# One scan over both values of a step instead of one for each, with doubled decay rows

## The chip, the cores and the metric

The kernel runs on one core of a Trainium2 chip. The time is the device time of one execution in microseconds (us); the figure given for a kernel is the median of its runs. The engines are called as in the profile: PE (TensorE, matrix products and transposes), DVE (VectorE), ACT (ScalarE), POOL (GpSimd, which here also starts the gathers and the weight loads) and SP (SyncE, which starts most other transfers). Each engine works through its own instructions in order.

## The reference, cut to what matters

The program computes two layers. Layer 0 adds to its input a mixer and a mixture of experts. The mixer, for B = 8 batches, T = 512 tokens and 16 heads of 16 keys by 16 values, is a recurrence that runs forward and backward over the tokens:

```python
def fwd_step(S, inp):
    rt, kt, vt, wt = inp
    S = jnp.exp(wt)[..., None] * S + kt[..., None] * vt[..., None, :]
    return (S, jnp.einsum('bhk,bhkv->bhv', rt, S))
def bwd_step(S, inp):
    rt, kt, vt, wt = inp
    y = jnp.einsum('bhk,bhkv->bhv', rt, S)
    S = jnp.exp(wt)[..., None] * (S + kt[..., None] * vt[..., None, :])
    return (S, y)
...
y = (y_f + y_b)   # then a gate, a norm over each head, a product with g and with Wo
```

The decay exp(wt) depends on batch, token and key, but not on the value index. Layer 1 (attention and a second mixture of experts) follows; no part of it is changed.

## The kernel before, in words

**The scans.** The state is laid out with 128 rows on the partitions (8 heads of 16 keys, two such halves c for the 256 keys of a batch) and the 512 tokens along the free axis. For one value index, a row is a linear recurrence along the tokens, which DVE's `tensor_tensor_scan` computes: out[t] = data0[t] * out[t-1] + data1[t]. The forward and the backward recurrence are joined: a first scan runs forward with factors `dq`, and a second runs over its result from the end with the factors `d`; `dq`, `d`, `q` and a changed `k` are made so that what comes out is the sum of both states.

**A step** (function `scans`) treats NV = 2 values of one half c of one batch; there are 8 x 2 x 8 = 128 steps. It multiplies the two value rows, which a transfer has spread over the partitions (`spread`, tile kv, 128 x 2 x 512, four buffers), by k (L901), scans each of the two rows forward (L910) and backward (L914), multiplies by r (L923), and leaves to PE the sum over the keys (L929, into the bank ys), which is issued for two steps at a time.

**Decays.** For each batch, `decays` computes d on ACT (two Exp, L829 and L830, 128 x 2 x 512 with one zero column behind each row), q on DVE (L835, L836), near on ACT (Ln L841, Exp L843) and dq on DVE (L848 to L854), and then multiplies k by q (L858). d and dq have two buffers each, so that the next batch's can be made while this one's are read.

**Order.** DVE, PE, ACT and SP take their instructions in the order in which the program issues them. That order is made by taking turns: every piece of work is a Python generator, and `Turns.turn` lets each issue its instructions up to its next `yield`. A step of the scans has four turns: L901; the two scans of the first row (and perhaps the sums for PE); the two scans of the second; L923. In the same turns the experts of layer 0 (39 chunks; g and u products L615, h on ACT L639 and on DVE L624, y L655, the turned inputs xsT L587 and L601), the projections and decays of the next batch (products m L732 and L734, their use xf on DVE L739 and POOL L742, the Ws L697) and the ending of the last one (L942 on: yg L950, yc L954, sq L957, var L965, sd L971 and L973, wide L976, rs L982, z L985 to L987, o L997) issue theirs. POOL's order is set by the scheduler instead. POOL also starts the weight loads wgu and wdn (L567), which wait until PE is done with the buffer, and the gathers xs (L577).

**Buffers in the way of the change.** `held(i, ...)` gives the tiles of a pool of numbered places with one buffer each. Places 0 to 7 first hold the normed inputs xn0 to xn7, later parts of the routing: `turn_round` makes for each of eight k a pair ls, hs (DVE L550, ACT L556) for PE's products L538 in four places each; batch 0's near lies in places 4 and 5. Layer 1 uses them again. PE's results of the projections, and the ending's var and rs, come out of the pool ps_rw with two banks; g, u, xsT and y out of ps_gu with four.

Of the kernel before, what the change touches and what calls it, by code (L numbers as in the profile page):

```python
# [26 lines left out]
F32 = mybir.dt.float32  # L27
I32 = mybir.dt.int32
AF = mybir.ActivationFunctionType
ALU = mybir.AluOpType  # L30
# [6 lines left out]
P = 128  # L37
# [128 lines left out]
def two_layers(ctx: ExitStack, tc: tile.TileContext, a: dict, out: bass.AP):  # L166
# [10 lines left out]
    def held(i, shape, name):  # L177
        return hold.tile(shape, F32, tag=f"held{i}", name=name)
# [193 lines left out]
    with ExitStack() as l0:  # L372
# [142 lines left out]
        def turn_round():  # L515


            n2 = NCH * NS
            parts = rw.tile([P, 5, NTT], F32, tag="x", name="parts")
            low, high, number = parts[:, 0:2], parts[:, 2:4], parts[:, 4]  # L520
            low, high = [[w[:, i] for i in range(2)] for w in (low, high)]
            whole = rw.tile([P, NTT], I32, tag="th", name="whole")
            for i in range(2):
                vec_e.tensor_scalar(whole, slot[i], P - 1, None, ALU.bitwise_and)
                vec_e.tensor_copy(low[i], whole)
                vec_e.tensor_scalar(whole, slot[i], 7, None, ALU.arith_shift_right)
                vec_e.tensor_copy(high[i], whole)
            vec_e.tensor_scalar(
                number, C["count"][:, :NTT], float(P), C["part"], ALU.mult, ALU.add
            )  # L530
            yield
            inv = ps_e.tile([P, n2], F32, tag="e", name="inv")
            last = None
            for k in range(NTT // 4 + 1):
                if last:
                    for j in range(4):
                        for i in range(2):
                            pe.matmul(  # L538
                                inv, last[0][:, i, j, :], last[1][:, i, j, :],
                                start=k == 1 and i + j == 0,  # L540
                                stop=k == NTT // 4 and (i, j) == (1, 3),
                            )
                    last = None
                if k < NTT // 4:
                    ls = held(k % 4, [P, 2, 4, P], f"ls{k}")
                    hs = held(4 + k % 4, [P, 2, 4, n2], f"hs{k}")
                    for i in range(2):
                        for o, of in ((ls, low), (hs, high)):
                            n = o.shape[3]
                            vec_e.tensor_tensor(  # L550
                                o[:, i], bc(of[i][:, 4 * k : 4 * k + 4], 2, n),
                                bc(C["count"][:, :n], 1, 4), ALU.is_equal,
                            )
                    for j in range(4):
                        n = 4 * k + j
                        act_e.activation(  # L556
                            hs[:, :, j, :], hs[:, :, j, :], AF.Copy, scale=number[:, n : n + 1]
                        )
                    last = ls, hs
                yield  # L560
            vec_e.tensor_copy(whose, inv)
            yield
# [106 lines left out]

        made = {}  # L670

        def projections(b):


# [13 lines left out]
            def mix(name, i, other=False):  # L688
                if other and first:
                    return held(i, [P, T], f"{name}_{b}")  # L690
                return rw.tile([P, T], F32, tag="xf", name=f"{name}_{b}", bufs=4)

            def project(w, xs, co, name, bank=bank):

# [111 lines left out]

            def decays():
                yield from until("inputs", b)
                d = rw.tile([P, NC, T + 1], F32, tag="d", name=f"d_{b}", bufs=2)
                vec_e.memset(d[:, :, T:], 0.0)  # L810
                dT = d[:, :, :T]
                xw, xr = yield from mixed(0, 3, other=True)
                ps = other_bank("dw")
                for c in range(NC):
                    pe.matmul(ps[:64, :], dw1[:, c, :], xw[c], start=c == 0, stop=c == NC - 1)
                yield
                act_e.activation(th[:64, :], ps[:64, :], AF.Tanh)
                r, pss = yield from projected(xr, 0, "r", other_bank)
                for co in range(NC):
                    act_e.copy(r[:, co, :], pss[co])  # L820
                pss = []
                for co in range(NC):
                    pss.append(other_bank(f"w{co}"))
                    pe.matmul(
                        pss[co], dw2[:, co * P : (co + 1) * P], th[:64, :], start=True, stop=True
                    )
                yield
                for co in range(NC):
                    act_e.activation(dT[:, co, :], pss[co], AF.Exp, bias=V("time_decay", co))  # L829
                act_e.activation(dT, dT, AF.Exp, scale=-1.0)  # L830
                for _ in range(1 if first else 2):
                    yield

                q = rw.tile([P, NC, T + 1], F32, tag="v", name=f"q_{b}", bufs=2)
                vec_e.tensor_scalar(q, d, 1.0, -1e-12, ALU.subtract, ALU.min)  # L835
                vec_e.scalar_tensor_tensor(q, d, 1.0, q, ALU.add, ALU.mult)  # L836
                yield

                near = [mix(f"near{c}", 4 + c, True) for c in range(NC)]
                for c in range(NC):  # L840
                    act_e.activation(near[c], q[:, c, :T], AF.Ln, scale=-1.0)  # L841
                for c in range(NC):
                    act_e.activation(near[c], near[c], AF.Exp, scale=-1.0)  # L843
                for _ in range(1 if first else 2):
                    yield
                dq = big("dq")
                for c in range(NC):
                    vec_e.tensor_tensor(dq[:, c, :], q[:, c, :T], near[c], ALU.mult)  # L848
                    vec_e.scalar_tensor_tensor(
                        dq[:, c, :], dq[:, c, :], 2.0, near[c], ALU.add, ALU.mult  # L850
                    )
                yield
                vec_e.scalar_tensor_tensor(dq, dq, -1.0, q[:, :, 1:], ALU.mult, ALU.mult)
                vec_e.tensor_tensor(dq, dq, dT, ALU.mult)  # L854
                yield
                yield from until("keys", b)
                k = made[b]["k"]
                vec_e.tensor_tensor(k, k, q[:, :, 1:], ALU.mult)  # L858
                made[b].update(d=d, dq=dq, r=r)
                done.add(("scans", b))  # L860
                yield
                (xg,) = yield from mixed(4)
                g, pss = yield from projected(xg, 3, "g")
                for co in range(NC):
                    act_e.activation(g[:, co, :], pss[co], AF.Silu)
                made[b]["g"] = g

            return inputs(), values(), decays()

        NV = 2  # L870
        STEPS = P // (P // HD) // NV

        def spread(b, c, vg):

            kv = rw.tile([P, NV, T], F32, tag="kv", name=f"kv{c}{vg}_{b}", bufs=4)
            for hh in range(P // HD):
                row = c * P + hh * HD + vg * NV
                nc.sync.dma_start(  # L878
                    kv[hh * HD : (hh + 1) * HD], bc(made[b]["vd"][row : row + NV, :], 0, HD)
                )  # L880
            return kv

# [2 lines left out]
        def scans(turns):  # L887
# [4 lines left out]
            for n, (b, c, vg) in enumerate(todo):  # L892
                if c == vg == 0:
                    x = rw.tile([P, NT, D], F32, tag="x", name=f"x_{b}")
                    z = rw.tile([P, NC, T], F32, tag="z", name=f"z_{b}")
                    if b + 1 < B:
                        turns.add(then(*projections(b + 1)))
                k, d, dq, r = (made[b][n] for n in ("k", "d", "dq", "r"))
                dc, qc, kc, rc = d[:, c, 1:], dq[:, c, :], k[:, c, :], r[:, c, :]
                kv = kvs.pop((b, c, vg))  # L900
                vec_e.tensor_tensor(kv, kv, bc(kc, 1, NV), ALU.mult)  # L901
                if vg == 0:
# [3 lines left out]
                if n + 1 == len(todo):  # L906
                    done.add(("spread",))
                yield
                for i in range(NV):
                    vec_e.tensor_tensor_scan(  # L910
                        out=kv[:, i, :], data0=qc, data1=kv[:, i, :], initial=0.0,
                        op0=ALU.mult, op1=ALU.add,
                    )
                    vec_e.tensor_tensor_scan(  # L914
                        out=kv[:, i, ::-1], data0=dc[:, ::-1], data1=kv[:, i, ::-1],
                        initial=0.0, op0=ALU.mult, op1=ALU.add,
                    )
                    if i == 0 and len(late) == 2:
                        for sums in late:
                            sums()  # L920
                        late = []
                    yield
                vec_e.tensor_tensor(kv, kv, bc(rc, 1, NV), ALU.mult)  # L923

                def sums(b=b, c=c, vg=vg, kv=kv, y=y, z=z, x=x):
# [618 lines left out]
```

## Time and profile before

| | us |
|---|---:|
| Median of 3 runs (2727.06 to 2733.11) | 2727.75 |
| The profiled execution | 2728.59 |
| Its span, first to last instruction | 2726.8 |
| DVE busy / PE busy / ACT busy / POOL busy in the span | 2157.0 / 2362.4 / 888.3 / 477.5 |
| First scan, last scan (start) | 99.8, 1421.2 |
| Scans L910 and L914 (512 of them), busy | 656.7 |
| The multiplies L901 and L923 (256 of them), busy | 334.9 |

The durations all come from the one profiled execution, so sums are made against its 2728.59 us. The scans fill about the first half of the execution, together with the experts of layer 0; after about 1480 us layer 1 runs. In the rows of the profile, "idle before" is the time in which an engine stood still ahead of a group of instructions, with what ended the wait; a busy PE is not PE at its peak, because the ends of its instructions are modelled.

### The profile page before, as it was taken

To read this page: it belongs to the slowest core of one execution; us is meant where nothing else is said; L and a number is where in the kernel's file an instruction comes from. 1 tells how busy PE (TensorE), PEld (TensorE's weight loads), DVE (VectorE), ACT (ScalarE), POOL (GpSimd) and SP (SyncE) were. 2 spreads that over 40 slices of the span, in tenths; PEclk is the share of its full clock that TensorE was granted. 3 is DMA by queue.
4 is the path that set the end of the run, shared out by engine and by line. 5 is a ranking of instruction groups with operands and counts; after the bars stand their busy time and mean duration, and the time that the engine had idled before them with its cause. 6 is when DMAs were issued, how large, how long until landed. Compare 5 with 4: busy or idle time off the path is not lost.

```text
span 2726.8 us, 32763 instructions
## 1 busy us (share of the span) xinstructions
PE 2362.4 (87%) x11900; PEld 1412.8 (52%) x11900; DVE 2157.0 (79%) x3063; ACT 888.3 (33%) x1687; POOL 477.5 (18%) x441
## 2 busy tenths in 40 slices
PE   6699898988989889898826899999989989898996
PEld 4355555555556545555503445555555555555554
DVE  7799999899999989989985755656576675756666
ACT  1233232222323123231102334434333434434344
POOL 2132232322223223232012100010010101001000
PEclk9688998989889899999957899999989989998998
DMA  6335455455465544655443100000010111000000
GB/s 219 112 104 148 141 176 148 142 146 156 138 176 153 158 133 138 173 151 140 138 122 104 43 16 17 20 27 25 20 36 20 32 32 31 25 24 21 20 9 17
DMA packets 100832, 248.87 MB, mean 91 GB/s; under 512 B 24992, under 2 KB 50368, under 8 KB 95552
## 3 DMA queue, kind: packets, MB, share of 16 engines
q1 hardware_dynamic: 70528, 113.32, 15.0%
q0 software_dynamic: 21168, 115.75, 13.6%
q10 hardware_dynamic: 8976, 17.69, 1.8%
q8 instruction: 96, 1.57, 0.2%
q14 instruction: 64, 0.52, 0.1%
HBM read 215.22 MB, written 31.46 MB: 90 GB/s over the span
## 4 chain that ended last, share of the span: by engine, by line
PE 57%; DVE 25%; DMA 6%; issue 6%; ACT 2%; SPq 2%; POOL 1%; DVEq 0%; ACTq 0%; POOLq 0%
PE y L1427 6%; PE y L655 6%; PE g L1381 5%; DMA kv<-vd 5%; PE g L615 4%; PE u L1381 4%; PE u L615 4%; DVE kv L910 3%; PE sc_g L1279 2%; DVE kv L901 2%; PE ys L929 2%; PE o_g L1307 2%; DVE kv L914 2%; PE qkv_l L1171 2%; SPq L878 2%
## 5 line engine op out<-in xcount | busy, mean ns | idle before, releaser
L914 DVE TENSOR_TENSOR_SCAN kv<-d,kv 128x512 f32<-128x512 f32 x256 | 336.7, 1315 | 8.8
L655 PE MATMUL y<-wdn,h 128*128 128x256 f32 x936 | 286.6, 443 | 54.9 <-DVE h L624 50.5
L910 DVE TENSOR_TENSOR_SCAN kv<-dq,kv 128x512 f32<-128x512 f32 x256 | 320.0, 1250 | 3.4
L655 PEld LDWEIGHTS y<-wdn,h 128*128 128x128 f32 x936 | 180.6, 211 | 186.6 <-issue 83.5
L1287 ACT ACTIVATE pt_g<-sc_g 128x512 f32<-128x512 f32 (+1 forms) x384 | 171.2, 531 | 275.0 <-PE sc_g L1279 215.3
L615 PE MATMUL g<-xsT,wgu 128*128 128x256 f32 x936 | 229.2, 388 | 4.7 <-ACT h L639 3.2
L1381 PE MATMUL g<-xT,w 128*128 128x512 f32 x384 | 203.7, 656 | 25.9 <-DVE att_l L1335 14.0
L615 PEld LDWEIGHTS g<-xsT,wgu 128*128 128x128 f32 x936 | 176.1, 192 | 57.4 <-issue 27.4
L1381 PE MATMUL u<-xT,w 128*128 128x512 f32 x384 | 188.5, 614 | 10.7 <-ACT qkT_g L1239 6.0
L615 PE MATMUL u<-xsT,wgu 128*128 128x256 f32 x780 | 196.3, 392 | 0.0
L1427 PE MATMUL y<-w,h 128*128 128x256 f32 x768 | 183.6, 392 | 0.7 <-ACT qkT_g L1239 0.7
L901 DVE TENSOR_TENSOR kv<-kv,k 128x1024 f32<-128x1024 f32 x128 | 172.0, 1344 | 6.6 <-DMA kv<-vd 6.6
L615 PEld LDWEIGHTS u<-xsT,wgu 128*128 128x128 f32 x780 | 149.5, 195 | 51.4 <-issue 22.8
L923 DVE TENSOR_TENSOR kv<-kv,r 128x1024 f32<-128x1024 f32 x128 | 162.9, 1273 | 3.6
L929 PE MATMUL ys<-kv,cst 128*32 128x512 f32 x512 | 105.7, 701 | 65.4 <-DVE kv L923 65.1
L1399 DVE TENSOR_TENSOR h<-h,u 128x512 f32<-128x512 f32 x96 | 66.0, 688 | 121.5 <-PE u L1381 116.6
L1427 PEld LDWEIGHTS y<-w,h 128*128 128x128 f32 x768 | 144.4, 193 | 34.2 <-issue 11.2
L639 ACT ACTIVATE h<-g 128x512 f32<-128x512 f32 (+1 forms) x117 | 61.7, 527 | 272.6 <-PE g L615 262.5
L1293 DVE TENSOR_TENSOR pt_g<-pt_g,cst 128x512 f32<-128x512 f32 x128 | 85.2, 686 | 75.1 <-ACT pt_g L1287 75.1
L742 POOL TENSOR_TENSOR xf<-xf,xnT 128x512 f32<-128x512 f32 x80 | 113.3, 1436 | 124.1 <-DVE xf L739 123.8
L1381 PEld LDWEIGHTS g<-xT,w 128*128 128x128 f32 x384 | 72.6, 201 | 110.7 <-issue 84.8
L1287 ACT ACTIVATE pt_l<-sc_l 128x384 f32<-128x384 f32 (+1 forms) x256 | 98.0, 469 | 86.3 <-PE sc_l L1279 70.7
(307 smaller groups left out, 3874.5 us busy)
## 6 DMA issues: line engine op xcount, KB each, us to landing
kv<-vd SPq DMA_DIRECT2D x1024, 64.0 KB
cb<-cd SPq DMA_DIRECT2D x128, 128.0 KB
outs<-ys POOLq DMA_DIRECT2D x39, 256.0 KB
w<-in_w ACTq DMA_DIRECT2D x12, 384.0 KB
xn<-in_x SPq DMA_DIRECT2D x8, 512.0 KB
xnT<-xT ACTq DMA_DIRECT2D x16, 256.0 KB
normed<-xn SPq DMA_DIRECT2D x8, 512.0 KB
xnT<-xnT SPq DMA_DIRECT2D x8, 512.0 KB
```

The lines of the kernel that those rows point to most:

```text
L615: pe.matmul(o, w[:, at + c * P : at + (c + 1) * P], xT[:, c, :], start=c == 0, stop=c == NC - 1,)
L655: pe.matmul(y[:, n, :], hs[j // 2][lo:, j % 2, n * P : (n + 1) * P], wd[lo:, j * D : (j + 1) * D], start=j == 0, stop=j == NJ0,)
L742: pool_e.tensor_tensor(t, t, xT[c], ALU.add)
L901: vec_e.tensor_tensor(kv, kv, bc(kc, 1, NV), ALU.mult)
L910: vec_e.tensor_tensor_scan(out=kv[:, i, :], data0=qc, data1=kv[:, i, :], initial=0.0, op0=ALU.mult, op1=ALU.add,)
L914: vec_e.tensor_tensor_scan(out=kv[:, i, ::-1], data0=dc[:, ::-1], data1=kv[:, i, ::-1], initial=0.0, op0=ALU.mult, op1=ALU.add,)
L923: vec_e.tensor_tensor(kv, kv, bc(rc, 1, NV), ALU.mult)
L929: pe.matmul(y[r0 : r0 + 32, :], C["take"][:, 24 - 8 * at : 56 - 8 * at], kv[:, i, :], start=at == 0, stop=at == 3, skip_group_check=True,)
L1287: act_e.activation(pt[:, i, :end], scs[i][:, :end], AF.Exp, scale=0.25)
L1293: vec_e.tensor_tensor(pt[:, :, a0 : a0 + m], pt[:, :, a0 : a0 + m], bc(mask[:, :m], 1, 4), ALU.mult,)
L1381: pe.matmul(ps, w[:, k, c * P : (c + 1) * P], xT[:, c, :], start=c == 0, stop=c == NC - 1,)
L1427: pe.matmul(y[:, i, :], hs[k][:, (t + i) * P : (t + i + 1) * P], w1[j - 5 + k][:, 2, :], start=k == 0, stop=k == 5,)
```

## The change

For each half c, the factor rows are copied twice, one behind the other, into tiles of 128 x 2 x 512 (`ds` from d, `dqs` from dq), by ACT. The kv tile of a step is then taken as one row of 1024, and one scan goes forward over it and one backward. Where the second value begins, the factor has to be zero: for the backward scan it is d's zero column, for the forward one POOL writes a zero into the first column of dq. The step keeps four turns: L901, the forward scan, the backward scan, L923. To make room, d and dq have one buffer each, ls and hs two places each, batch 0's near lies in places 0 and 1, and ds and dqs lie in places 4 to 7 for even batches, and in places 1 and 2 and two tiles of their own for odd ones.

```diff
                 if k < NTT // 4:
-                    ls = held(k % 4, [P, 2, 4, P], f"ls{k}")
-                    hs = held(4 + k % 4, [P, 2, 4, n2], f"hs{k}")
+                    ls = held(k % 2, [P, 2, 4, P], f"ls{k}")
+                    hs = held(2 + k % 2, [P, 2, 4, n2], f"hs{k}")
...
+            def twice(name):
+                out = []
+                for c in range(NC):
+                    n = 2 * (name == "dqs") + c
+                    if b % 2 == 0:
+                        out.append(held(4 + n, [P, NV, T], f"{name}{c}_{b}"))
+                    elif n < 2:
+                        out.append(held(1 + n, [P, NV, T], f"{name}{c}_{b}"))
+                    else:
+                        out.append(rw.tile([P, NV, T], F32, tag=f"dqs{c}", name=f"{name}{c}_{b}"))
+                return out
...
-                d = rw.tile([P, NC, T + 1], F32, tag="d", name=f"d_{b}", bufs=2)
+                d = rw.tile([P, NC, T + 1], F32, tag="d", name=f"d_{b}")
...
                 act_e.activation(dT, dT, AF.Exp, scale=-1.0)
+                ds = twice("ds")
+                for c in range(NC):
+                    act_e.copy(ds[c], bc(d[:, c, 1:], 1, NV))
...
-                near = [mix(f"near{c}", 4 + c, True) for c in range(NC)]
+                near = [mix(f"near{c}", c, True) for c in range(NC)]
...
-                dq = big("dq")
+                dq = big("dq", 1)
...
                 vec_e.tensor_tensor(dq, dq, dT, ALU.mult)
-                yield
+                pool_e.memset(dq[:, :, 0:1], 0.0)
+                yield
+                dqs = twice("dqs")
+                for c in range(NC):
+                    act_e.copy(dqs[c], bc(dq[:, c, :], 1, NV))
                 yield from until("keys", b)
...
-                for i in range(NV):
-                    vec_e.tensor_tensor_scan(
-                        out=kv[:, i, :], data0=qc, data1=kv[:, i, :], initial=0.0,
-                        op0=ALU.mult, op1=ALU.add,
-                    )
-                    vec_e.tensor_tensor_scan(
-                        out=kv[:, i, ::-1], data0=dc[:, ::-1], data1=kv[:, i, ::-1],
-                        initial=0.0, op0=ALU.mult, op1=ALU.add,
-                    )
-                    if i == 0 and len(late) == 2:
-                        for sums in late:
-                            sums()
-                        late = []
-                    yield
+                flat = kv.rearrange("p v t -> p (v t)")
+                vec_e.tensor_tensor_scan(
+                    out=flat, data0=qc, data1=flat, initial=0.0, op0=ALU.mult, op1=ALU.add
+                )
+                if len(late) == 2:
+                    for sums in late:
+                        sums()
+                    late = []
+                yield
+                vec_e.tensor_tensor_scan(
+                    out=flat[:, ::-1], data0=dc[:, ::-1], data1=flat[:, ::-1],
+                    initial=0.0, op0=ALU.mult, op1=ALU.add,
+                )
+                yield
```

More of the change, by code (lines that the diff above doesn't have):

```diff
@@ L670, in two_layers @@
         made = {}
+        NV = 2
+        STEPS = P // (P // HD) // NV
         def projections(b):
@@ L858, in decays @@
                 vec_e.tensor_tensor(k, k, q[:, :, 1:], ALU.mult)
-                made[b].update(d=d, dq=dq, r=r)
+                made[b].update(ds=ds, dqs=dqs, r=r)
                 done.add(("scans", b))
@@ L868, in projections @@
             return inputs(), values(), decays()
-        NV = 2
-        STEPS = P // (P // HD) // NV
         def spread(b, c, vg):
@@ L897, in scans @@
                         turns.add(then(*projections(b + 1)))
-                k, d, dq, r = (made[b][n] for n in ("k", "d", "dq", "r"))
-                dc, qc, kc, rc = d[:, c, 1:], dq[:, c, :], k[:, c, :], r[:, c, :]
+                k, ds, dqs, r = (made[b][n] for n in ("k", "ds", "dqs", "r"))
+                dc, qc = (x[c].rearrange("p v t -> p (v t)") for x in (ds, dqs))
+                kc, rc = k[:, c, :], r[:, c, :]
                 kv = kvs.pop((b, c, vg))
```

## The prediction

> **What bounds the kernel now.** I read the page's summary first, then its 40 slices, then the costliest groups, and after these the waits and the order of time inside the stage that the change touches. Ahead of each view I say what to look for.
>
> The busy times by engine, then the slices of PE and DVE and the clock of PE:
>
> ```profile
> PE 2362.4 (87%) x11900; PEld 1412.8 (52%) x11900; DVE 2157.0 (79%) x3063; ACT 888.3 (33%) x1687; POOL 477.5 (18%) x441
> ...
> PE   6699898988989889898826899999989989898996
> ...
> DVE  7799999899999989989985755656576675756666
> ...
> PEclk9688998989889899999957899999989989998998
> ```
>
> PE has the larger total, but DVE stands at 8 and 9 tenths from slice 3 to slice 21 (110 to 1430 us) and at 5 to 7 after that. The first stretch is layer 0's scans, the second is layer 1, which has no scan. The change lies wholly in the first. By stretches of 200 us (busy us of PE, PEld, DVE, ACT, POOL, with the instructions of each):
>
> ```profile
> 600.00:800.00 200.00, 183.12 (x700) 114.88 (x700) 188.24 (x189) 53.25 (x83) 52.86 (x46) 0.91 0.54 155
> 800.00:1000.00 200.00, 176.24 (x665) 108.36 (x664) 187.91 (x186) 57.07 (x86) 59.38 (x50) 0.92 0.49 142
> ```
>
> DVE is 94% busy, PE 88 to 92% with modelled ends, ACT under 30%. What DVE does there (busy us, mean ns of one, idle before):
>
> ```profile
> L914 DVE TENSOR_TENSOR_SCAN kv<-d,kv 128x512 f32<-128x512 f32 x256 | 336.7, 1315 | 8.8
> ...
> L910 DVE TENSOR_TENSOR_SCAN kv<-dq,kv 128x512 f32<-128x512 f32 x256 | 320.0, 1250 | 3.4
> ```
>
> The 512 scans are 656.7 us, half of the 1320 us. What DVE waited for from 200 to 1300 us (total, times, longest):
>
> ```profile
> DVE xf L739 <- PE m L732: 32.7, 10, 6.3
> DVE h L624 <- PE u L615: 7.4, 6, 1.8
> ```
>
> About 41 us in 1100, all on PE. So DVE sets the pace, except in some stretches of each batch in which PE is behind; that matters below.
>
> [...] It has one scan of 8 elements (minimum, median and maximum ns):
>
> ```profile
> L477 DVE TENSOR_TENSOR_SCAN chto<-one,ch x1: 174/174/174, 106.0 to 106.0; 128x8 f32<-128x8 f32 x1
> ...
> L914 DVE TENSOR_TENSOR_SCAN kv<-d,kv x256: 1224/1224/2214, 101.0 to 1421.2; 128x512 f32<-128x512 f32 x128
> ```
>
> (1224 - 174) / 504 = 2.083 ns an element; the plain multiplies L901 and L923 do 1024 elements in about 1.22 us, half of that per element. What is left is 174 - 8 x 2.083 = 157 ns fixed. [...] the scan at 395.5 us beside a POOL add took 1.93 us instead of 1.22.
>
> **The change part by part.**
>
> *Scans.* 512 scans of 512 elements become 256 of 1024. An estimate from the two rows: 174 + 1016 x 2.083 = 2291 ns. A pair cost 2448 ns, so 157 ns are saved 256 times: 40.2 us. Beside the durations there is what lies between instructions. In order of time on DVE (start, duration):
>
> ```profile
> 382.82 1.22 DVE L910 TENSOR_TENSOR_SCAN kv<-dq,kv 128x512 f32<-128x512 f32 x1
> 384.08 1.23 DVE L914 TENSOR_TENSOR_SCAN kv<-d,kv 128x512 f32<-128x512 f32 x1
> 385.22 1.20 DVE L853 SCALAR_TENSOR_TENSOR dq<-dq,q 128x1024 f32<-128x1024 f32 x1
> 386.45 1.23 DVE L854 TENSOR_TENSOR dq<-dq,d 128x1024 f32<-128x1024 f32 x1
> ```
>
> The backward scan needs the forward one and starts 1.26 us after it, 0.03 past its end; L853 needs neither and starts 1.14 after, 0.08 before the end. The instruction order of the two programs gives the count. Before: 361 scans are followed by what needs them (256 forward ones, 105 backward ones ahead of L923), 151 by something else. After: 131 and 125, because the turn's end now lies between forward and backward and other work comes between in 102 of 128 steps. 361 x 0.03 - 151 x 0.08 = -1.3 us; 131 x 0.03 - 125 x 0.08 = -6.1 us: another 4.8. Together **45 us less on DVE**, 0.35 a step.
>
> *What of that reaches the end.* Each batch of some 171 us has stretches in which PE is behind and DVE waits for it, for example 6.3 us at 485 and 4.7 us at 516, where projections and expert products fall together. In the chain of waits PE runs nearly unbroken from about 460 to 520 us. What DVE saves in such a stretch only lengthens the wait at its end. That is 60 of 171 us, about a third: **15 us lost, 30 kept.** The bounds are none lost (45) and nearly all.
>
> *Copies.* Four copies of 128x1024 a batch on ACT, 32 in all. The nearest row is the Exp L830 over 1024 elements, 1.06 us: 34 us of ACT time, 2.1 us at two places a batch. ACT idles two thirds of the stage, so the work itself costs nothing; the place matters. ds stands right behind the Exp; the next step on that path, Ln (L841), waits for DVE's q (L835, L836), which takes longer than the two copies. dqs is worse: ACT runs ahead of DVE, and at dqs it must now wait for L854 and for the zero behind it. In batch 2, first PE's two m products, then ACT's h, sd and h, in order of time:
>
> ```profile
> 384.80 1.12 PE L734 MATMUL m<-th,m2b 32*128 32x512 f32 x2
> ...
> 387.77 1.12 PE L734 MATMUL m<-th,m2b 32*128 32x512 f32 x2
> ```
> ```profile
> 382.98 0.60 ACT L639 ACTIVATE h<-g 128x512 f32<-128x512 f32 x1
> ...
> 384.89 0.29 ACT L971 ACTIVATE sd<-var,geps 128x32 f32<-128x32 f32 x1
> ...
> 387.88 0.60 ACT L639 ACTIVATE h<-g 128x512 f32<-128x512 f32 x1 [1.40 <-PE g L615]
> ```
>
> The new order puts dqs ahead of all three. L854 ends at 387.7; zero and copies end near 390.2; with two table loads of 1.28 us between, h comes at 391.5 and sd at 393.4, each 8.5 us late. sd frees the bank of var, one of the two banks of ps_rw, and the second m product (387.77) takes that bank: PE, in order, stands until about 393.7, 6 us. In batches 3 and 6 the same working gives 8.4 us (zero behind the gathers of xs on POOL, which end at 562.4; second m from 559.1 to 567.5); in 1, 4 and 7 under 1 us. So PE falls 29 us behind in total over seven batches. But DVE does not need these results soon: it takes h at 397.3, the second m at 397.9, the next u at 403.0. I put 0.5 us a batch on what reaches DVE, **3 us lost**; bounds 0 and the whole 9 us of ACT's hold a batch (the slower rival).
>
> *Zero.* Eight POOL memsets of 2 elements, the nearest row being L749, 0.10 us. In the order they stand ahead of the blocked weight loads, not behind them, except for the xs gathers just named.
>
> *Buffers.* d, dq with one buffer: the next batch writes them over 100 us after the last reader; nothing. near, ds and dqs in held tiles of batch 0: the inputs in them were stored and transposed by 80 us; nothing. ls and hs with two buffers instead of four: a comparison k must wait for PE's products of k - 2. At k = 6, DVE started at 150.7 and those products ended about 151.0; at k = 7, 153.8 against 154.7: 1.5 us; bounds 0 and 4. Start: v's copies and its store move back by the ds copies, 0.8 us on the way to the first scan. Together **2.5 us**.
>
> *Not moved:* SP's queue and POOL's order otherwise (two entries change places). [...] the adds wait up to 1 us more each, in stretches where PE is late this can reach PE: 0 to 5 us, I take 1.
>
> Sum: -45 + 15 + 3 + 2.5 + 1 = -23.5. The profiled execution took 2728.59 us (span 2726.8 and 1.8 around it): 2705.1. The median shown is 0.8 lower, so **2704 us**.
>
> **Rivals.**
> - *DVE keeps nearly all.* PE is shifted by an earlier DVE too, since its gaps wait on L923 and L624: then little is lost and it ends near 2685. For it: DVE's own idle time is only 41 us. Against: the waits at m recur in every batch. 0.17.
> - *PE takes over.* PE's late stretches grow as DVE gets faster, the 45 us come back as waits at L739 and L624: 2724 to 2728. For: PE at 88 to 92%. Against: those ends are modelled, and DVE hardly ever waits outside the m stretches. 0.08.
> - *Slower: ACT's hold at dqs.* ACT stands about 9 us in each of seven batches behind L854, and with it h, xsT, sd and through var's bank PE. If DVE waits for all of it, 63 us are added to the 26.5 saved otherwise: 2764. It decides from 3.8 us of DVE waiting a batch. For: the bank. Against: DVE takes these results 6 us and more later. 0.05.
> - *The long scan isn't cheaper.* If fixed cost follows length, 2448 ns stay; with the order's 4.8 saved and 6.5 lost: 2730. Two sizes of scan speak against it. 0.02.
>
> **How the numbers follow.** The likeliest case has 0.68 and its own range is 2694 to 2716. From 2684 (all 45 kept) to 2724 (PE bound) less than 2 in 10 is left out. A measurement of this kernel tells apart about 0.2%, 5.5 us. Faster by more than that: 0.68 and 0.17, and a quarter of PE's case, 0.87; within it: the rest of PE's case and part of the long scan's, 0.08; slower 0.05.
>
> **What would show it.** Scans of 2.29 us, 256 of them, and DVE busy in total about 40 us less, right or wrong to within 5. Copies near 1.06 us on ACT. ACT idle ahead of dqs, released by POOL or DVE; PE idle ahead of the second L734 product of batches 2, 3, 5 and 6. DVE's waits for PE up by 15 us or so. Wrong would be scans of 2.4 us or more, DVE waiting on h or m for over 4 us a batch behind dqs, or a layer 1 stage longer than before.

## The result: a quarter of the gain that was forecast

| | before | after |
|---|---:|---:|
| Median of 8 runs, us | 2727.66 (2726.74 to 2733.11) | 2722.19 (2716.99 to 2728.95) |
| Ratio to before, 95% interval | | 0.9978 [0.9967, 0.9988] |
| The profiled execution, us | 2728.59 | 2728.95 (the longest of its eight) |

The change takes 5.5 us off; 23.5 were forecast. The measured time lies inside the range, near its upper end, and at the bound that the prediction had set for telling a change from none. The trace of the change is of its longest execution, 6.8 us over the median, so differences between the two traces can be some us larger than those of the medians.

The page of the kernel after: the span, the busy times by engine, and the slices of PE and DVE.

```profile
span 2727.2 us, 32561 instructions
...
PE 2360.6 (87%) x11900; PEld 1413.5 (52%) x11900; DVE 2119.3 (78%) x2807; ACT 918.8 (34%) x1719; POOL 540.4 (20%) x449
...
PE   6599888988989888898826899999989989898996
...
DVE  7789979799898988989985755656576675756666
```

DVE does 37.7 us less than before (2157.0), as forecast, and PE the same as before. But DVE's row now has dips to 7 and 8 in layer 0 where it had 9. What DVE saved came back as idle time. By stretches of 200 us, in the columns used for the kernel before:

```profile
600.00:800.00 200.00, 181.74 (x689) 113.70 (x688) 185.53 (x149) 55.49 (x85) 62.90 (x50) 0.92 0.55 162
800.00:1000.00 200.00, 176.67 (x674) 110.51 (x673) 179.56 (x149) 62.56 (x92) 66.78 (x46) 0.91 0.49 146
```

From 800 to 1000 us DVE is busy 179.6 us instead of 187.9. The groups of the step on DVE (busy us, mean ns of one, idle before and what ended it):

```profile
L942 DVE TENSOR_TENSOR_SCAN kv<-ds,kv 128x1024 f32<-128x1024 f32 x128 | 307.2, 2400 | 1.5
...
L934 DVE TENSOR_TENSOR_SCAN kv<-dqs,kv 128x1024 f32<-128x1024 f32 x128 | 299.5, 2340 | 2.8
...
L925 DVE TENSOR_TENSOR kv<-kv,k 128x1024 f32<-128x1024 f32 x128 | 174.0, 1359 | 23.7 <-DMA kv<-vd 23.5
```

The scans take 606.7 us instead of 656.7. Ahead of the first multiply of a step DVE now stands idle for 23.7 us over the span, all but 0.2 of it on the transfer that spreads the values. In the kernel before it was 6.6 us:

```profile
L901 DVE TENSOR_TENSOR kv<-kv,k 128x1024 f32<-128x1024 f32 x128 | 172.0, 1344 | 6.6 <-DMA kv<-vd 6.6
```

That one wait lies near the end of the scans (step 123, at 1385 us), and the change has it too. The rest is new. From 200 to 1300 us, DVE's waits (total, times, longest):

```profile
DVE xf L755 <- PE m L748: 33.5, 9, 7.4
DVE h L624 <- PE u L615: 20.0, 15, 3.1
DVE kv L925 <- DMA kv<-vd: 15.3, 4, 7.3
```

The row of L925 has no counterpart among the waits of before in this stretch. The row of h grew from 7.4 to 20.0 us.

### The profile page after: what moved, and what is told of

Read it like the earlier page. It is cut to its first block, busy times and chain, and to the rows that moved or that the text cites. A ratio compares the mean times of both kernels' runs of the same rounds, so it can differ in the third digit from the quotient of the medians.

```text
span 2727.2 us, 32561 instructions
## 1 busy us (share of the span) xinstructions
PE 2360.6 (87%) x11900; PEld 1413.5 (52%) x11900; DVE 2119.3 (78%) x2807; ACT 918.8 (34%) x1719; POOL 540.4 (20%) x449
## 4 chain that ended last, share of the span: by engine, by line
PE 56%; DVE 21%; issue 8%; DMA 7%; ACT 3%; POOL 2%; SPq 2%; DVEq 0%; ACTq 0%; POOLq 0%
PE y L1451 6%; PE g L1405 5%; DMA kv<-vd 5%; PE g L615 5%; PE y L655 4%; PE u L1405 4%; PE u L615 4%; PE sc_g L1303 2%; DVE kv L925 2%; PE ys L953 2%; PE o_g L1331 2%; DVE kv L942 2%; DVE kv L934 2%; PE qkv_l L1195 2%; SPq L899 2%
## 5 line engine op out<-in xcount | busy, mean ns | idle before, releaser
L655 PE MATMUL y<-wdn,h 128*128 128x256 f32 x936 | 276.7, 433 | 39.2 <-DVE h L624 34.6
L942 DVE TENSOR_TENSOR_SCAN kv<-ds,kv 128x1024 f32<-128x1024 f32 x128 | 307.2, 2400 | 1.5
L934 DVE TENSOR_TENSOR_SCAN kv<-dqs,kv 128x1024 f32<-128x1024 f32 x128 | 299.5, 2340 | 2.8
L925 DVE TENSOR_TENSOR kv<-kv,k 128x1024 f32<-128x1024 f32 x128 | 174.0, 1359 | 23.7 <-DMA kv<-vd 23.5
L947 DVE TENSOR_TENSOR kv<-kv,r 128x1024 f32<-128x1024 f32 x128 | 168.5, 1316 | 3.6
L758 POOL TENSOR_TENSOR xf<-xf,xnT 128x512 f32<-128x512 f32 x80 | 129.1, 1634 | 84.9 <-DVE xf L755 84.6
L577 POOL DMA_INDIRECT xs<-normed,whose x78 | 119.7, 1535 | 73.6 <-DVE whose L561 47.2
```

Source lines behind the costliest of these rows:

```text
L577: pool_e.indirect_dma_start(out=xs[:, n, :], out_offset=None, in_=normed, in_offset=bass.IndirectOffsetOnAxis(ap=whose[:, at : at + 1], ax ...
L655: pe.matmul(y[:, n, :], hs[j // 2][lo:, j % 2, n * P : (n + 1) * P], wd[lo:, j * D : (j + 1) * D], start=j == 0, stop=j == NJ0,)
L758: pool_e.tensor_tensor(t, t, xT[c], ALU.add)
L934: vec_e.tensor_tensor_scan(out=flat, data0=qc, data1=flat, initial=0.0, op0=ALU.mult, op1=ALU.add)
L942: vec_e.tensor_tensor_scan(out=flat[:, ::-1], data0=dc[:, ::-1], data1=flat[:, ::-1], initial=0.0, op0=ALU.mult, op1=ALU.add,)
```

## The experiments

Three explanations stood at first. **Hold**: ACT's wait for dqs, or the copies, costs more than the 3 us forecast. **Port**: the longer scans slow POOL's adds and gathers, and these PE; the name stands for a shared port, which the author assumed and no run shows. **PE**: PE had no room, and the time that DVE saved turns into waits for it. A fourth, the **completion of a transfer**, came out of the traces later.

### The parts of the change one at a time

Everything but the long scan (copies, buffers, zero; four scans of 512 over the halves of the doubled rows):

```diff
-                vec_e.tensor_tensor_scan(out=flat, data0=qc, data1=flat, ...)
...
+                for i in range(NV):
+                    vec_e.tensor_tensor_scan(out=kv[:, i, :], data0=qc[:, i, :], ...)
+                    vec_e.tensor_tensor_scan(out=kv[:, i, ::-1], data0=dc[:, i, ::-1], ...)
```

> All of the change except the long scan: copies, zero, buffers and tiles as in the changed kernel, but four scans of 512 a step over the two halves of the doubled rows, in the turns of the kernel before. DVE has the same scans as before (656 us). Theory 'hold' (ACT stands at dqs behind L854, PE behind var's bank, and what DVE saves is lost there): slower than before by 15 to 25 us. Theory 'PE' (PE with its own waits sets the length of a batch, so a DVE saving finds no use): slower by 0 to 8 us, from the start of batch 0 and 1 and the held bank. Theory 'port' [...]: within 4 us of before, since the scans are short again.

Measured 2729.63 us, ratio to before 1.0006 [1.0, 1.0012]. Copies, hold and buffers together cost 1.7 us here, 3.3 at the end of the interval; Hold had asked for 15 to 25.

The dqs copies of batches 1 to 7 issued four turns later, behind the fifth product m:

```diff
                 dqs = twice("dqs")
-                for c in range(NC):
-                    act_e.copy(dqs[c], bc(dq[:, c, :], 1, NV))
+                if first:
+                    for c in range(NC):
+                        act_e.copy(dqs[c], bc(dq[:, c, :], 1, NV))
...
                 (xg,) = yield from mixed(4)
+                if not first:
+                    for c in range(NC):
+                        act_e.copy(dqs[c], bc(dq[:, c, :], 1, NV))
```

> The changed kernel with the two dqs copies of batches 1 to 7 issued four turns later, behind the m products of the last mix, so that ACT no longer waits there and sd frees var's bank in time. Theory 'hold': 2700 to 2706, that is 16 to 22 us below the changed kernel. Theories 'PE' and 'port': 2716 to 2722. PE's wait for sd ahead of the second m product (26.9 us in the changed kernel) should go to about zero under each of them.

Measured 2723.62 us, 0.999 [0.9979, 1.0]: the same as the change itself. In its trace PE no longer waits for sd, and the end does not move.

The rows of batch 0 used for all batches (28 copies and 7 zeros left out):

```diff
-                ds = twice("ds")
-                for c in range(NC):
-                    act_e.copy(ds[c], bc(d[:, c, 1:], 1, NV))
+                if first:
+                    ...
+                    made["rows"] = ds, dqs
+                else:
+                    ds, dqs = made["rows"]
```

> The changed kernel with ds and dqs made for batch 0 alone, and read by the scans of all batches: 28 copies and 7 zeros are left out. Long scans without copies. Theory 'hold': 2698 to 2705. Theories 'PE' and 'port': 2714 to 2722, at or a little below late_copies.

Measured 2720.01 us, 0.9971 [0.9959, 0.9983]. With hardly a copy left, the gain is 8 us (the kernel before, run beside it, took 2727.96), little more than the change's 5.5. The hold and the copies are not where the forecast went.

The kernel before with two places each for ls and hs:

```diff
-                    ls = held(k % 4, [P, 2, 4, P], f"ls{k}")
-                    hs = held(4 + k % 4, [P, 2, 4, n2], f"hs{k}")
+                    ls = held(k % 2, [P, 2, 4, P], f"ls{k}")
+                    hs = held(2 + k % 2, [P, 2, 4, n2], f"hs{k}")
```

> The kernel before with two places each for ls and hs instead of four, nothing else. By the prediction's term 1 to 2 us slower than before; if the changed kernel's delay of 6 us between its steps 4 and 8 came from these buffers, 5 to 6 us slower; if that delay came from POOL's adds beside long scans, within 2 us of before.

Measured 2728.19 us, 1.0002 [0.9994, 1.001]: nothing that can be told from no change.

### Less work for PE, less for POOL

Both kernels with half of the products g and u of layer 0's experts, and both without POOL's 80 adds of xnT:

```diff
-                    for c in range(NC):
+                    for c in range(1):
                         pe.matmul(o, w[:, at + c * P : at + (c + 1) * P], xT[:, c, :], ...)
```
```diff
-                        pool_e.tensor_tensor(t, t, xT[c], ALU.add)
```

> The kernel before with half of the expert products g and u of layer 0 left out (the second half of the sum over 256 inputs), some 43 of 100 of PE's expert matmuls less. DVE has the same work. It is the base for after_light. Theory 'PE': faster than before by 20 us or more, since PE is often late. A DVE bound all through would give 5 us or less.

> The changed kernel with the same products left out as in before_light. Theory 'PE': the scans' saving now shows, 30 to 45 us below before_light. Theories 'hold' and 'port': as small a difference as in full, 3 to 15 us[...].

> The kernel before with POOL's 80 adds of xnT (L742) left out, so that the mixed inputs lack that term; DVE's and PE's work is the same. The base for after_noadd. A few us to 20 us faster than before, since scans and multiplies stretched by a POOL add (some 50 us on DVE in all) go back to their own length.

> The changed kernel with the same adds left out. Theory 'port': 25 us or more below before_noadd. Theory 'PE' and theory 'hold': 3 to 12 us below before_noadd, as in the full pair.

Then both edits together:

> The kernel before with both cuts: half of the expert products g and u left out, and POOL's adds of xnT left out. The base for after_light_noadd. 2685 to 2695.

> The changed kernel with both cuts. Theory 'PE': with PE lighter and the adds' hop over POOL gone from PE's stretches, the long scans save 30 to 42 us against before_light_noadd. If a limit other than PE's load (the transfers of kv, DVE's own order) holds it: 0 to 20 us.

| | before, us | after, us | after less before |
|---|---:|---:|---:|
| as they are | 2727.66 | 2722.19 | -5.5 |
| light | 2724.10 | 2701.65 | -22.5 |
| without adds | 2695.41 | 2697.66 | +2.3 |
| light, without adds | 2676.44 | 2644.27 | -32.2 |

I read the second row first as support for PE: with a lighter PE the forecast gain is there. But PE had also asked that the kernel before get 20 us faster with half of the products gone, and it got 3.5 faster. PE was also lightened by less than the edit suggests, because its granted clock was lower in these runs: 0.887 in the middle for the light kernel before, 0.916 for the kernel before. The third row speaks against Port: without the adds, the long scans gain nothing, where Port had asked for 25 us; the 3 to 12 us that PE and Hold had asked for did not come either. Both bases without the adds came out faster than was expected of them (2695.41, 12 us beyond the 20 that were allowed; 2676.44 for 2685 to 2695). The table has a simpler reading, which came later: the pairs that gain are those in which *both* kernels wait for the spread. In the traces of the light pair, DVE's waits from 200 to 1300 us hold, before and after in turn,

```profile
DVE kv L901 <- DMA kv<-vd: 11.3, 5, 4.7
```
```profile
DVE kv L925 <- DMA kv<-vd: 13.2, 5, 4.6
```

while of the pair without adds only the kernel with long scans has such a row (13.1 us, longest 6.9).

### The saving alone, without the change

The kernel before, with its scans over 472 of the 512 elements: an estimate from the 2.083 ns an element gives 512 x 40 x 2.083 ns = 42.7 us less on DVE, with nothing else moved.

```diff
+                    part, qs, ds = kv[:, i, :472], qc[:, :472], dc[:, :472]
                     vec_e.tensor_tensor_scan(
-                        out=kv[:, i, :], data0=qc, data1=kv[:, i, :], initial=0.0,
+                        out=part, data0=qs, data1=part, initial=0.0,
...
-                        out=kv[:, i, ::-1], data0=dc[:, ::-1], data1=kv[:, i, ::-1],
+                        out=part[:, ::-1], data0=ds[:, ::-1], data1=part[:, ::-1],
```

> The kernel before with each of its 512 scans over 472 of the 512 elements: 40 x 2.083 ns = 83 ns less each, 43 us less on DVE, and no other difference: no long scan, no copies, no zero, the same buffers. Theory 'PE' (DVE's saving finds no use because PE's stretches set the end of each batch): 4 to 12 us faster than before. A theory by which the long scan or what came with it spends the gain: 25 to 40 us faster.

Measured 2700.89 us, 0.9899 [0.9884, 0.9914]; the kernel before, run beside it, took 2727.61. So 26.7 of 42.7 us reach the end, 63%. That is the share which the prediction had, and far from none. DVE's waits in this kernel:

```profile
DVE xf L739 <- PE m L732: 34.7, 10, 6.5
DVE h L624 <- PE u L615: 7.8, 7, 2.2
...
DVE kv L901 <- DMA kv<-vd: 0.2, 1, 0.2
```

There is next to no wait for the spread, and h stands where it stood before. With nearly the same work on DVE (busy 2116.3 us here, 2119.3 in the change), this kernel and the change differ by 21 us. So PE's own load is not what takes the missing 21 us: the long scan, or something that came with it, is.

The late copies with the 80 adds on DVE instead of POOL:

```diff
-                            pool_e.tensor_tensor(t, t, xT[c], ALU.add)
+                            vec_e.tensor_tensor(t, t, xT[c], ALU.add)
```

> late_copies with the 80 adds of xnT on DVE instead of POOL: DVE gets 80 x 0.69 = 55 us of work, of which it had some 30 us of waiting for PE to fill and loses the stretching of its own instructions beside POOL's adds; PE gets its mixed inputs a hop earlier. If POOL's adds are what makes both engines late: 2700 to 2712. If DVE's room is only inside PE's stretches: 2720 to 2735.

Measured 2734.72 us, 1.0026 [1.0016, 1.0035]. Taking the 80 adds off POOL does not bring the gain back; what they cost on DVE outweighs it. Whether the effect called Port has a small price of its own is not told by this run: its trace also holds the wait which the next section is about.

### The transfer that DVE waits for

In the trace of the kernel after, DVE stops once in batch 2 for 7.3 us. In order of time (start, duration, in brackets idle before):

```profile
348.33 1.23 DVE L947 TENSOR_TENSOR kv<-kv,r 128x1024 f32<-128x1024 f32 x1
349.51 0.06 DVE L826 MEMSET d<- 128x2 f32 x1
356.90 1.23 DVE L925 TENSOR_TENSOR kv<-kv,k 128x1024 f32<-128x1024 f32 x1 [7.33 <-DMA kv<-vd]
```

L925 at 356.90 is step 22, and the spread of step 22 consists of eight transfers that SP issues. SP's own waits from 345 to 358 us:

```profile
SPq L899 <- DMA vd<-v: 7.7, 1, 7.7
```

SP waits for the store of v, which belongs to the *next* batch, to another buffer, and starts on ACT's queue:

```profile
344.16 0.58 ACT L811 COPY v<-v 128x512 f32<-128x512 f32 x1 [0.33 <-PE v L713]
344.78 0.37 ACTq L813 DMA_DIRECT2D vd<-v  x1
```

No data runs from that store to step 22. What joins them is seen in the instruction order of the two programs, with the waits, and the traces hold the same order of semaphores. In both programs the transfers of SP and of ACT take eight completion semaphores, DMAHW0 to DMAHW7, in turn, and each waits for the landing of the last transfer that took its own; here SP waits 7.7 us for that of the store. SP's rows for step 22, before and then after:

```
198 L878 DMACopy kv_1_1991<-vd_1128 16x1024 [waits DMAHW0_49,PE_49]
199 L878 DMACopy kv_1_1991<-vd_1128 16x1024 [waits DMAHW2_49]
...
205 L878 DMACopy kv_1_1991<-vd_1128 16x1024 [waits DMAHW0_49]

198 L899 DMACopy kv_1_1967<-vd_1127 16x1024 [waits DMAHW1_49,PE_49]
199 L899 DMACopy kv_1_1967<-vd_1127 16x1024 [waits DMAHW2_49]
...
205 L899 DMACopy kv_1_1967<-vd_1127 16x1024 [waits DMAHW0_49]
```

The rows stand at the same numbers, 198 to 205: SP's order did not change. The numbers of the semaphores did. Before, the store had DMAHW1, between the first and second transfer of this step. The next to wait for it is the first transfer of step 23, which is in no hurry. After, the store has DMAHW0, ahead of all eight, and the next to wait for it is the last transfer of step 22 itself. Seven of the eight are issued from 338.2 to 341.5 us, the eighth at 349.6, once the store has landed. Step 70 has the same pair of patterns (4 6 7 0 1 2 3 4 before, 5 6 7 0 1 2 3 4 after), and DVE stood 5.9 us there at 851.8. Why the long scan gave the store another number was not followed.

Elsewhere a transfer that is held by the store cost DVE little. In both kernels the store also holds one transfer in the spreads of steps 6, 38, 54, 86 and 102, for 3.8 to 14 us, and DVE stops there for 1.9 us at most.

Which kernels have which pattern fits with all runs so far, though this was seen after they had run. The one of before is in copies_only, two_places, before_472 and before_noadd; the one of after is in late_copies, one_copy, after_noadd, dve_adds and in both kernels of both light pairs (there the store has DMAHW7 or DMAHW3, and it holds the seventh transfer of the step).

The test moves the store. In batches 1 to 7 it is issued behind the k products of the same batch, some three turns later:

```diff
                 vd = dram.tile([D, T], F32, tag="vd", name=f"vd_{b}")
-                act_e.dma_start(vd.rearrange("(c p) t -> p c t", p=P), v)
+                if first:
+                    act_e.dma_start(vd.rearrange("(c p) t -> p c t", p=P), v)
                 yield
...
                 for co in range(NC):
                     act_e.mul(k[:, co, :], pss[co], -1.0)
+                if not first:
+                    act_e.dma_start(vd.rearrange("(c p) t -> p c t", p=P), v)
```

The move was made in the kernel after, in the kernel before, and in the kernel with the late copies:

> The changed kernel with the store of v (vd) of batches 1 to 7 issued by ACT after the k copies, about three turns later than in the changed kernel, and nothing else. With that the store takes a completion semaphore between two transfers of a step's spread, so that the wait for the store falls on the next step's spread instead of the last transfer of steps 22 and 70 (and 6, 38, 54, 86, 102). Theory 'semaphore' (the changed kernel loses its gain where a transfer of kv waits for the store of v, whose semaphore it shares): 2700 to 2712, DVE's wait for kv 3 us or less. Theory 'PE' alone: 2718 to 2724, with the wait for kv gone and waits for PE longer instead.

> The kernel before with the same move of the store. Its transfers of steps 22 and 70 did not wait for the store before either, and DVE waited for kv only once, behind the expert stage. Both theories: within 5 us of before. It is the base for vd_last.

> The changed kernel with both the late dqs copies and the late store of v. If ACT's hold costs something once the wait for kv is gone: 3 to 8 us below vd_last. If not: within 3 us of it.

| store moved in | median, us | ratio to before, 95% | without the move |
|---|---:|---:|---:|
| after | 2702.33 | 0.9913 [0.9896, 0.9929] | 2722.19 |
| before | 2726.81 | 0.9999 [0.9991, 1.0007] | 2727.66 |
| late copies | 2707.29 | 0.9923 [0.991, 0.9936] | 2723.62 |

The move is worth nothing in the kernel before and 20 us in the kernel after (16 with late copies), as the semaphore's theory had it. The third kernel was expected within 3 us of the first or below it, and its median is 5 us above; their intervals overlap. The semaphores of step 22 are now 0 1 2 4 5 6 7 0: the store sits between the third and the fourth, and the wait has moved: it now holds the third transfer of step 23, from 334.4 to 347.4 us, and DVE does not stop for it. The page, and DVE's waits, of the kernel after with the store moved:

```profile
span 2698.0 us, 32554 instructions
...
PE 2343.6 (87%) x11900; PEld 1405.8 (52%) x11900; DVE 2118.0 (79%) x2807; ACT 919.4 (34%) x1719; POOL 533.6 (20%) x449
```
```profile
DVE xf L755 <- PE m L748: 40.4, 10, 7.4
DVE h L624 <- PE u L615: 10.6, 9, 2.1
```

No row for kv, h nearly back, and DVE as busy as in the kernel after; the wait at xf is 6.9 us longer than there. From L901 or L925 of step 8 to that of step 112, added up from the traces (us):

| | length | DVE busy | DVE idle |
|---|---:|---:|---:|
| before | 1080.8 | 1021.2 | 59.5 |
| before, scans over 472 | 1056.9 | 989.0 | 68.0 |
| after | 1077.6 | 989.0 | 88.6 |
| after, store moved | 1055.7 | 987.0 | 68.7 |
| before, store moved | 1080.9 | 1015.9 | 64.9 |

DVE's work in this stretch fell by 32 us in the change, and 29 of them became idle time. Of these, 8 to 9 also appear where only the scans are shorter; there the waits for PE from 200 to 1300 us rose by 7.2 us in all. The other 20 go when the store is moved. The two kernels with the same work on DVE and next to no wait of DVE for a spread agree to 1.2 us in length.

The two stops themselves are 13.2 us long. They are more costly than that, because PE is slower behind them. DVE's xf, which stands behind the late multiply, comes late, and PE stands idle for 4.8 us until it has it. In the 20 us from the multiply of step 22 on, in the kernel after, before, and after with the store moved (columns as in the stretches above; the third number from the end is PE's granted clock):

```profile
356.00:376.00 20.00, 17.04 (x48) 9.07 (x49) 18.73 (x13) 2.08 (x4) 10.72 (x6) 0.74 0.49 133
```
```profile
346.00:366.00 20.00, 20.00 (x79) 11.60 (x78) 18.45 (x18) 2.96 (x5) 8.57 (x6) 1.00 0.67 197
```
```profile
341.00:361.00 20.00, 20.00 (x80) 11.99 (x79) 17.79 (x15) 3.73 (x7) 11.73 (x7) 1.00 0.66 198
```

PE issues 48 matrix products instead of 79 or 80. Behind step 70 the clock is 0.91 in the kernel after and 1.00 in the two others. In the traces of all 17 kernels it is 0.66 to 0.91 behind both steps in the nine that have the pattern of after, and 1.00 in the eight that don't. An estimate from these figures: 7.3 and 5.9 us of stops, 0.26 x 20 and 0.09 x 20 us of PE's clock, together 20 us. That they add up to the whole may be chance, since PE sets DVE's pace only in part.

The granted clock of whole runs goes the same way: its median is 0.917 in the change and 0.9215 with the store moved, and within the latter the run at 0.915 took 2712.36 us and the one at 0.924 took 2696.32. The two runs of the change at 0.915 took 2725.36 and 2728.95. So at a like clock, with one run against two, the move is worth some 13 to 17 us, and the rest of the 20 goes with the clock.

This version, the change with the store moved, is faster than both kernels: 2702.33 us, 25.5 under before.

## Why the prediction was right or wrong

- **Scans: right.** Forecast 2291 ns. The single line of each scan, with minimum, median and maximum:

```profile
L934 DVE TENSOR_TENSOR_SCAN kv<-dqs,kv x128: 2225/2291/3062, 100.6 to 1417.7; 128x1024 f32<-128x1024 f32 x128
```

  Backward it is 2285. The estimate from the scan of 8 and the scan of 512 elements held to within 6 ns. DVE's total fell by 37.7 us, forecast 40 to within 5. That this fits is in part luck: the scans gave 50.0 us, 10 more than the 40.2 forecast for them, and the multiplies L925 and L947 took 7.6 back (334.9 to 342.5).
- **A third lost to PE: right in size, the mechanism shown in part.** Shorter scans alone kept 63%. DVE's waits for PE at xf and h came to 51.0 us in the kernel with the store moved, 40.1 before: up 11, forecast 15. With shorter scans these two rose by 2.4 us only, and all waits for PE by 7.2, so that about half of the 16 us which were lost there is not found in waits for PE. The reading behind the third was rough as well: a batch takes 166 us (104 steps in 1080.8), not 171, and in the chain of waits DVE, not PE, stands from 491 to 500 us.
- **Copies: right.** 1043 ns for dqs and 1047 for ds in the median, forecast 1.06 us, and the work lies beside DVE's.
- **ACT's hold: right in its place, too high in its price.** PE waited four times for sd, and in the trace of the kernel after that is, from 200 to 1300 us,

```profile
PE m L750 <- ACT sd L995: 26.9, 4, 8.3
```

  against a forecast of 29 us with 8.4 the longest. The term for the end was 3 us. Late copies took the wait away and the end stayed (2723.62 against 2722.19; with the store moved in both, 2707.29 against 2702.33). So no cost of the hold is seen at the end, and the term is about 0. The slower rival had described a real wait, and it had said from which point it decides: that point was not reached.
- **Buffers: too high.** 1.5 us for two places of ls and hs; measured 0.5 over the kernel before, with an interval that takes in no change. The start came out as forecast: the first scan starts 0.8 us later (100.6 against 99.8).
- **Port: not resolved.** 1 us was taken, for adds that wait up to 1 us more each; both were the author's estimates. The longest of the 80 adds took 3203 ns in the change against 2134 before, the median 1096 against 1110 (L758, L742). POOL's busy time rose by 62.9 us. The gathers' issue, with minimum, median and maximum, before and after:

```profile
L577 POOL DMA_INDIRECT xs<-normed,whose x78: 945/1008/1794, 160.6 to 1279.5; - x78
```
```profile
L577 POOL DMA_INDIRECT xs<-normed,whose x78: 942/1408/2797, 160.7 to 1283.2; - x78
```

  That is 0.4 us more in the median. The kernel with the store moved carries this too, and it gains 25.5 us, so little of it can reach the end.
- **The step that failed: "Not moved: SP's queue".** The term was put at nothing because SP's instructions keep their order. They do. But the eight completion semaphores go to the transfers of SP and ACT alike, and with the long scan the store of v took one that was a place earlier, twice. The move of the store gave 20 us back, where forecast and result lie 18 apart. The prediction priced SP's queue by its order alone; the waits in the same list of instructions would have shown 1 2 3 4 5 6 7 0 where the kernel before has 0 2 3 4 5 6 7 0.
- **The rival that came nearest, for the wrong reason.** "PE takes over" gave 2724 to 2728 and names waits at L739 and L624. The wait at L624 did grow, by 12.6 us, but with the stops of DVE and the lower clock of PE behind them: with the store moved it is 10.6 in all. The case that the prediction took as likeliest is what the change does once that wait is gone: 2702 for a forecast of 2704. To meet within 2 us is luck in part, since of the 6.5 us that the sum allowed for hold, buffers and port next to nothing was found.
- **Open.** The move of the store changes both the semaphore and the time of the store; no run changed the number of the semaphore alone. The direct waits are 7.3 and 5.9 us; the lower clock of PE behind them, which the traces show, is large enough for the rest of the 20, but no run tests it alone. In the profiled execution of the change, and with the rows of batch 0 alone, step 8 also starts 6 us later than before (212.8 against 206.4); with the late copies (206.1) or the store moved (205.6) it does not. No run isolates that.

## What to carry to other kernels

A change that leaves a queue's order alone can still change which completion semaphore a transfer takes; here the store of v ahead of step 22 took DMAHW0 instead of DMAHW1. Where a multiply waits for one transfer of several and that transfer waits for one it shares no data with, look at the semaphores in the waits of the issuing engine, and move the stranger to another turn (worth 20 us here). And when a gain stays away, make the same saving in the old kernel by other means: shorter scans showed in one run that the room was there, and that the loss lay in the long scan or in something that came with it. Look at PE's granted clock behind a stop, too: here a wait of 7.3 us was followed by 20 us at a clock of 0.74, and one of 5.9 us by 20 us at 0.91.

## What the runs showed of the hardware

- The scans of 8, 512 and 1024 elements took 174, 1224 and 2291 ns in the median (L477 and L914 before, L934 after). The first two give 157 ns and 2.083 ns an element, and by these 1024 elements take 2290 ns: in these scans the fixed part was paid once and not by length. The one scan of 256 elements (L468) took 692 ns in the kernel before without the adds, 690 by this sum, but 1353 ns with them, when an add of POOL ran beside it (L742, from 103.67 to 104.76 us).
- A store and a spread that share no data were coupled through a completion semaphore. The store was issued at 344.78 us and let the eighth transfer go at 349.6, 4.8 us later; that transfer was done 7.3 us after its issue. No run shows what made either of them take that long.
- PE's granted clock was lower behind a stop: behind the two waits it was 0.66 to 0.91 over 20 us in nine kernels (0.74 and 0.91 in the kernel after), and 1.00 at the same steps in the eight without them.
- POOL's 80 adds were worth 32 us in the kernel before (2695.41 without them, ratio 0.9879 [0.9865, 0.9894]), though POOL is busy 18% of the span. Moved to DVE, with late copies in both, they cost 11 us more than on POOL (2734.72 against 2723.62).
